# A graph-attention and top-two expert network on one core: one store of routed rows becomes two, and the order of the last work changes

## The chip, the core and the metric

The kernel runs on one core of a Trainium2 chip. The core has five engines that each work through their own list of instructions in order and wait for one another through semaphores: TensorE (PE, with its weight loads shown as PEld), VectorE (DVE), ScalarE (ACT), GpSimd (POOL) and SyncE (SP). SP, ACT and POOL can start DMAs; only POOL starts the indirect ones here, whose rows are addressed by a list of indices. The metric is the device time of one execution in microseconds.

## The reference

The input x has 64 batches of 256 tokens with 256 features, all in f32. Two layers follow each other. Layer 0 is a graph attention with 4 heads over one 256x256 adjacency matrix, and a linear layer. Layer 1 is a graph attention with one head, and a mixture of experts:

```python
x = x + gnn0(layernorm(x), adj)          # 4 heads of 64, leaky relu, masked softmax, elu
x = x + layernorm(x) @ weight.T + bias
x = x + gnn1(layernorm(x), adj)          # one head of 256, relu
t = layernorm(x)                         # tokens of the mixture of experts, 16384 x 256
probs = softmax(t @ router_w.T)          # 8 experts
rw, re = top_k(probs, 2); rw = rw / rw.sum()
x = x + t + sum_e combine[:, e] * (gelu(t @ w1[e] + b1[e]) @ w2[e] + b2[e])
```

Each token needs only the two experts that it chose, so 2 of 8 products have to be computed.

## The kernel before

**Batches.** `batch_layers` handles one batch: both attentions, the linear layer, the norms and the router's logits (the last PE work of a batch, `pl`, L771). A loop at the end of the kernel starts a new batch every three steps and lets all jobs that are alive advance in each step by a rank that they yield. So the order of instructions on each engine is fixed when the program is built. The first instruction of ACT in a batch (L471) and its four matmuls (L463) mark the pace.

**Routing.** The first 61 batches are *routed*, in chunks of 4 batches (eleven times), 2 (seven times) and 1 (three times). For each chunk `route` finds the two best experts of each token (`top_two`), counts by two matmuls (`pp`, L1199 and L1200) how many rows each expert has received so far, and so gives each (token, choice) a row in a store in HBM, `xs`. This store has eight regions, one per expert. `send` (L1155) writes the token's row there with an indirect DMA of POOL, twice per 128 tokens: once for the first choice, once for the second. A row has 260 columns: 256 features, the token's number, the first choice's expert, and the two numbers from which the weight follows.

**Pairs.** A *pair* is two tiles of 128 rows of one region. `allot` decides on DVE which regions have a full pair and writes expert and place of each next pair to a small table; SP, PE and DVE read it into registers. `expert_pair` then runs one pair: SP loads the expert's first weights (`we`, 264 KB, L977), the rows (`xr`, four DMAs, L987) and the last columns (`xt`, L998); DVE turns the rows (L117), PE computes the first product (`ph`, L1050) and ACT the gelu (L1056); DVE picks the weight by comparing the expert's number (L1026, L1030); PE computes the second product (`py`, L1066), DVE adds the bias (L1077) and ACT multiplies by the weight (L1042). The loop starts these jobs from a list, at most about two per batch until late in the kernel.

**Adding.** `scatter` (L1088) adds each of the pair's two tiles to the rows of the output with an indirect, accumulating DMA of POOL. A token's first and second choice may lie in pairs that follow each other, and two accumulating DMAs must not touch one row at the same time. So both scatters of a pair wait for the two of the pair before it (`before = added[-2:] + based`; `based` are the plain stores of the routed batches, which must land first).

**The end.** As a full pair is only certain when a region has 256 rows, E - 1 = 7 pairs are held back. Behind the last chunk `allot_rest` gives out 14 pairs, 10 whole and 4 of one tile; a block of zero rows (`fill`) is written behind each region's last row so that these pairs have defined rows. In all 129 pairs with 254 tiles are computed. The last three batches are not routed but *dense*: `dense_expert` runs all eight experts on a batch, and DVE adds each result by its weight to the batch's sum (L1125), which SP stores (L1136). Their 24 steps are laid between the pairs, in two groups (batch 61, then 62 and 63), and their first weights come from HBM (L1113).

**POOL** also computes the reciprocal roots of the norms (L400, L401, L438, L441), in order with sends and scatters.

**Until batch 18** (`SETTLED`) the layer-0 input is turned by PE and the attention terms of layer 1 by PE too; later DVE and DMAs do this.

## Time and profile before

| | |
|---|---|
| median of 17 runs | 1470.78 us (1466.56 to 1474.3) |
| the profiled execution | 1472.71 us |
| its span, first to last instruction | 1470.6 us |
| mean granted clock of TensorE | 0.985 |
| scatters (L1088) | 254, 407.5 us of POOL |
| sends (L1155) | 244, 256.4 us of POOL |
| product matmuls of experts (L1050, L1066) | 1224 + 1208 records, 280.6 + 282.5 us of PE |
| DMA traffic | 235.14 MB, mean 160 GB/s |

The profile is one execution. Busy time of an engine is the time in which it ran an instruction; register, branch and semaphore instructions are not in it. A PE matmul in f32 shows as two records. "Idle before" in a row is the time that the engine stood still before those instructions, with the work that ended last ahead of them. The clock is the share of full speed that the throttle granted to TensorE.

### The profile page before, as it was taken

The numbers are of one execution on the slowest core, as the hardware profiler recorded it, in microseconds if no ns is written. First come the engines' busy times: TensorE is split into PE (matmuls) and PEld (weight loads), VectorE is DVE, ScalarE is ACT, GpSimd is POOL, SyncE is SP. The second block draws the span as 40 slices with busy tenths as digits, with TensorE's granted clock in tenths as the row PEclk, the third lists the DMA queues.
The fourth block names the chain that finished last, engine by engine and source line by source line (L and its number), as shares of the span: only waits on it lengthen the run. The fifth ranks groups of instructions, "written<-read, shape, count | busy, mean of one in ns | idle before, by whom it ended". The sixth has DMA issues, their size and how long they took to land. (4 is left out here: it accounts for less than half of the span.)

```text
span 1470.6 us, 29780 instructions
## 1 busy us (share of the span) xinstructions
PE 1406.9 (96%) x8030; PEld 1250.9 (85%) x8030; DVE 1235.8 (84%) x4357; ACT 1002.7 (68%) x2385; POOL 856.2 (58%) x849
## 2 busy tenths in 40 slices
PE   6899999999999999999999999999999999889995
PEld 5698888899999999999999999888888888678884
DVE  7789999989998989899999989999888987775443
ACT  1477667677778777777777777766878787653431
POOL 2122446355867676676758585676666677644443
PEclk9899999999999999999999999999999999999998
DMA  4822243567777767787777677668687876799532
GB/s 126 247 81 87 91 131 117 141 163 172 203 182 190 179 165 180 181 196 186 191 170 188 158 196 182 182 166 206 156 197 156 184 158 142 151 224 198 87 44 43
DMA packets 356969, 235.14 MB, mean 160 GB/s; under 512 B 244796, under 2 KB 320068, under 8 KB 356804
## 3 DMA queue, kind: packets, MB, share of 16 engines
q1 hardware_dynamic: 304464, 157.46, 40.6%
q0 software_dynamic: 48288, 65.81, 23.4%
q10 hardware_dynamic: 4052, 9.98, 2.3%
q8 instruction: 66, 1.08, 0.3%
q14 instruction: 99, 0.81, 0.2%
HBM read 145.72 MB, written 87.41 MB: 159 GB/s over the span
## 5 line engine op out<-in xcount | busy, mean ns | idle before, releaser
L1088 POOL DMA_INDIRECT out_dram<-y,xt x254 | 407.5, 1604 | 224.1 <-issue 64.2
L589 PE MATMUL pv<-q,z 128*128 128x65 f32 (+1 forms) x2560 | 363.0, 297 | 0.2
L589 PEld LDWEIGHTS pv<-q,z 128*128 128x128 f32 x2560 | 332.8, 193 | 13.9 <-DVE z L575 0.4
L1155 POOL DMA_INDIRECT xs<-xng,pos x244 | 256.4, 1051 | 65.3 <-issue 58.7
L1066 PE MATMUL py<-w2s,hT 128*128 (+1 forms) x1208 | 282.5, 384 | 5.0 <-ACT hT L1056 5.0
L1066 PEld LDWEIGHTS py<-w2s,hT 128*128 128x128 f32 x1208 | 228.1, 192 | 38.5 <-ACT hT L1056 8.7
L575 DVE SCALAR_TENSOR_TENSOR z<-z,q,mask 128x256 f32<-128x256 f32 x504 | 231.8, 482 | 13.2 <-DMA z<-terms 4.2
L1050 PE MATMUL ph<-sT,we 128*128 128x256 f32 (+1 forms) x1032 | 237.6, 379 | 4.6 <-DVE sT L117 1.7
L1050 PEld LDWEIGHTS ph<-sT,we 128*128 128x128 f32 x1032 | 193.3, 192 | 32.8 <-ACT q L506 2.9
L1042 ACT ACTIVATE y<-y,w 128x256 f32<-128x256 f32 x254 | 111.5, 498 | 114.1 <-DVE y L1077 113.9
L453 ACT COPY xT<-pt 128x512 f32<-128x512 f32 x209 | 121.3, 587 | 84.4 <-PE pt L447 72.5
L400 POOL TENSOR_SCALAR rstd<-mv 128x4 f32<-128x4 f32 (+1 forms) x67 | 15.9, 238 | 212.0 <-DVE mv L378 165.3
L418 ACT ACTIVATE off<-x,sums 128x256 f32<-128x256 f32 x256 | 129.4, 505 | 14.1 <-DVE x L672 8.5
L498 PE MATMUL pq<-wx,xT 128*128 128x259 f32 x512 | 126.1, 389 | 5.4 <-ACT xT L453 5.4
L463 PE MATMUL pq<-wx,xT 128*128 128x268 f32 x512 | 129.3, 396 | 2.1 <-DVE xT L117 0.8
L665 PE MATMUL pf<-wfT,xT 128*128 128x256 f32 x512 | 122.9, 383 | 0.0
L1077 DVE TENSOR_TENSOR y<-py,b2s 128x512 f32<-128x512 f32 (+1 forms) x129 | 84.9, 677 | 44.0 <-PE py L1066 36.2
L1056 ACT ACTIVATE hT<-ph,we 128x256 f32<-128x256 f32 (+1 forms) x258 | 103.3, 469 | 24.4 <-issue 11.2
L463 PEld LDWEIGHTS pq<-wx,xT 128*128 128x128 f32 x512 | 98.7, 193 | 21.8 <-DVE wx L168 1.4
L498 PEld LDWEIGHTS pq<-wx,xT 128*128 128x128 f32 x512 | 96.9, 192 | 22.7 <-ACT xT L453 8.4
L711 ACT ACTIVATE rel<-pv,rinv 128x256 f32<-128x256 f32 x128 | 54.0, 470 | 87.2 <-DVE rinv L596 86.7
L665 PEld LDWEIGHTS pf<-wfT,xT 128*128 128x128 f32 x512 | 93.9, 194 | 10.5 <-ACT xT L453 0.2
(191 smaller groups left out, 2357.2 us busy)
## 6 DMA issues: line engine op xcount, KB each, us to landing
we<-wpack SPq DMA_DIRECT2D x129, 264.0 KB
xr<-xs SPq DMA_DIRECT2D x500, 64.0 KB
z<-terms SPq DMA_DIRECT2D x46, 512.0 KB
xin<-in_x_dram SPq DMA_DIRECT2D x64, 256.0 KB
out_dram<-base SPq DMA_DIRECT2D x61, 256.0 KB
xblk<-in_x_dram SPq DMA_DIRECT2D x188, 64.0 KB
z<-terms ACTq DMA_DIRECT2D x17, 512.0 KB
z<-terms SPq DMA_DIRECT2D x46, 128.0 KB
```

What stands on the lines that cost most here:

```text
L418: nc.scalar.activation(off, src[:, t, :], AF.Square, bias=sums[:, t : t + 1], scale=-float(D), accum_out=sq[:, at + t : at + t + 1],)
L453: nc.scalar.copy(dst, pt)
L463: nc.tensor.matmul(pq.rearrange("p h c -> p (h c)"), xT[:, k, t * P : (t + 1) * P], wx[:, k, :], start=(k == 0), stop=(k == KT - 1),)
L498: nc.tensor.matmul(pq, xT[:, k, t * P : (t + 1) * P], wx1[:, k, :], start=(k == 0), stop=(k == KT - 1),)
L575: nc.vector.scalar_tensor_tensor(z[:, j, :, h, :], terms, q[:, j, h, HD + 2 : HD + 3], masks[0][:, j, :].rearrange("p (t i) -> p t i", t=N ...
L589: nc.tensor.matmul(pv[:, h, :], z(j, h, t), q[:, j, h, : d + 1], start=(j == 0), stop=(j == NT - 1),)
L665: nc.tensor.matmul(pf[:, t, :], xT[:, k, t * P : (t + 1) * P], wfT[:, k, :], start=(k == 0), stop=(k == KT - 1),)
L1042: nc.scalar.activation(y[:, t, :], y[:, t, :], AF.Copy, scale=w[:, t : t + 1])
L1050: nc.tensor.matmul(ph[:, f, :], we[:, k * D + f * P : k * D + (f + 1) * P], xT[:, k, :], start=(k == 0), stop=(k == KT - 1),)
L1066: nc.tensor.matmul(py[:, t, :], hT[:, f, t * P : (t + 1) * P], w2s[:, e, f * D : (f + 1) * D].rearrange("p e c -> p (e c)"), start=(f == 0 ...
L1088: d = nc.gpsimd.indirect_dma_start(out=out_rows, out_offset=bass.IndirectOffsetOnAxis(ap=xt[:, t, 0:1].bitcast(I32), axis=0), in_=y[:, t, ...
L1155: d = nc.gpsimd.indirect_dma_start(out=xs_d[: E * CAP * PAIR, :], out_offset=bass.IndirectOffsetOnAxis(ap=at, axis=0), in_=xe, in_offset=None,
```

## The change

Each choice gets a store of its own, `xs0` and `xs1`, with eight regions each. All tokens' first choices lie in one, all second ones in the other. As each token occurs once in each store, the pairs of one store never share a row: their scatters no longer wait for each other, and only where the choice changes does a scatter wait for those of the other choice. The order in which the two choices are worked through alternates from chunk to chunk, so there is one such change per chunk. A pair's weight lies ready in the row, so the two DVE instructions that picked it are gone; the token's number is written to two columns instead of one.

Each store holds back 7 pairs. There are 62 routed batches and 2 dense ones (one more chunk of 1). Per store 54 pairs are given out as they fill and 15 at the end, 11 whole and 4 of one tile: together 138 pairs with 268 tiles. The filling rows now carry numbers of tokens of the two dense batches, in two columns that alternate between pairs, and are added as zeros; so the scatters of the 30 last pairs wait for both dense stores, and for the last pair but one.

The dense steps begin as soon as a dense batch is routed, two per step of the loop, ahead of the last 30 pairs. The eight experts' first weights are loaded once into the memory that held the attention's z (`bring_home`); dense steps read them there, and each of the last 30 pairs gets its copy by DVE instead of a DMA from HBM. `PAIRED` and `SETTLED` grow by one chunk (to 15 and 22).

```diff
-    CHUNKS = (4,) * 11 + (2,) * 7 + (1,) * 3
+    CHUNKS = (4,) * 11 + (2,) * 7 + (1,) * 4
-    CAP = ROUTED * NT * P // PAIR + 1
+    CAP = ROUTED + 1
+    R = 2 * E
-    PAIRED = CHUNKS[0] + CHUNKS[1] + 3
-    SETTLED = CHUNKS[0] + CHUNKS[1] + CHUNKS[2] + CHUNKS[3] + 2
+    PAIRED = sum(CHUNKS[:3]) + 3
+    SETTLED = sum(CHUNKS[:5]) + 2
...
-    xs_d = tc.dram_tile([(E * CAP + 1) * PAIR, ROW], F32, name="xs")
+    xs_d = [tc.dram_tile([(E * CAP + 1) * PAIR, ROW], F32, name=f"xs{k}") for k in range(2)]
...
-        fill[:, :, D : D + 1].bitcast(I32), pattern=[[1, 2], [1, 1]], base=0,
+        fill[:, :, D : D + 2].bitcast(I32), pattern=[[1, 2], [PAIR, 2]], base=ROUTED * N,
...
-    region = iota([E], [[CAP, E]], 0, 0, "region")
+    region = iota([R], [[0, 2], [CAP, E]], 0, 0, "region")
...
-        z = work.tile([P, NT, NT, H, P], F32, tag="z4", name="z4", bufs=2)
+        z = zbig[:, b % 2]
...
-    def expert_pair(j, n, ids, ef, regs, needs, tiles=2):
+    def expert_pair(k, j, n, ids, regs, needs, tiles=2, at_home=False):
...
-        d = nc.sync.dma_start(
-            out=we, in_=wpack[bass.ds(e_sp, 1), :, :].rearrange("e p c -> (e p) c")
-        )
+        if not at_home:
+            nc.sync.dma_start(
+                out=we, in_=wpack[bass.ds(e_sp, 1), :, :].rearrange("e p c -> (e p) c")
+            )
...
+        if at_home:
...
+            e = bass.ds(regs["copy"][i], 1)
+            nc.vector.tensor_copy(we[:, :C_B1], w1s[:, e, :].rearrange("p e c -> p (e c)"))
+            nc.vector.tensor_copy(
+                we[:, C_B1 : C_B1 + KT], b1s[:, e, :].rearrange("p e c -> p (e c)")
+            )
...
-        nc.vector.scalar_tensor_tensor(
-            w[:, :tiles, None], xt[:, :tiles, 1:2], ef[:, j : j + 1], xt[:, :tiles, 2:3],
-            op0=ALU.is_equal, op1=ALU.mult,
-        )
-        nc.vector.tensor_tensor(
-            w[:, :tiles, None], w[:, :tiles, None], xt[:, :tiles, 3:4], ALU.add
-        )
...
-            nc.scalar.activation(y[:, t, :], y[:, t, :], AF.Copy, scale=w[:, t : t + 1])
-        scatters.append((y, xt))
+            nc.scalar.activation(
+                y[:, t, :], y[:, t, :], AF.Copy, scale=xt[:, t, 2 + k : 3 + k]
+            )
+        scatters.append((k, y, xt, at_home))
...
-        y, xt = scatters.pop(0)
-        before = added[-2:] + based
+        k, y, xt, padded = scatters.pop(0)
+        before = list(based)
+        at = len(rest) % 2
+        if padded:
+            before += [ins for some in rest[-2:-1] for ins in some]
+            rest.append([])
         based.clear()
+        if k != turn[0]:
+            turn[0] = k
+            before += added[1 - k]
+            added[k].clear()
...
-    GROUPS = [range(ROUTED, ROUTED + 1), range(ROUTED + 1, B)]
+    GROUPS = [[b] for b in range(ROUTED, B)]
+    stored = []
+
+    w1s = zbig.rearrange("p a i j h q -> p (a i j h q)").rearrange("p (e c) -> p e c", e=E)
+    b1s = const.tile([P, E, KT], F32, tag="b1s", name="b1s")
+
+    def bring_home():
+
+        for e in range(E):
+            nc.sync.dma_start(
+                out=w1s[:, e, :].rearrange("p (k f) -> p k f", k=KT),
+                in_=w1[e].rearrange("(p k) f -> p k f", p=P),
+            )
+            if e % 2:
+                yield 99
+        nc.sync.dma_start(
+            out=b1s, in_=wpack[:, :, C_B1 : C_B1 + KT].rearrange("e p c -> p e c")
+        )
+        yield 99
...
-            hT = hidden(own["xT"], we)
+            hT = hidden(own["xT"], w1s[:, e, :], b1s[:, e, :])
...
+        stored.append(b)
+        based.append(d.ins)
...
-        m = rt([E, nt], "m")
-        tt(m.rearrange("p e t -> p t e"), ohs[:, 0], ohs[:, 1], ALU.add)
+        m = rt([2, E, nt], "m", 1)
+        vec.tensor_copy(m.rearrange("p k e t -> p k t e"), ohs)
...
+        order_of = (1, 0) if c % 2 else (0, 1)
+        for k in order_of:
             regs = {}
...
+            for j in range(REST if last else n):
+                waiting.append(
+                    lambda k=k, j=j, regs=regs: expert_pair(
+                        k, j, REST if last else n, ids, regs, needs,
+                        1 if last and j >= WHOLE else 2, last,
+                    )
+                )
...
-    FLUSH = 2 * (E - 1)
+    LEFT = ROUTED - max(ROUTED - CHUNKS[-1] - (E - 1), 0)
+    REST = LEFT + E - 1
...
-            done += nt
-            n = max(done - (E - 1) - taken, 0) if b < ROUTED else 0
+            done += nb
+            n = max(done - (E - 1) - taken, 0) if b + nb < ROUTED else 0
...
-                if waiting and len(scatters) < 3:
+                if waiting and len(scatters) < 5:
...
-            if dense_jobs and step >= dense_free:
-                units, job = dense_jobs.pop(0)
-                pairs = waiting or any(a[2].__name__ == "expert_pair" for a in active)
-                dense_free = max(dense_free, step - 0.5) + units * (1.25 if pairs else 0.5)
-                begin(job(), 90)
-            if scatters:
+            for _ in range(2):
+                if dense_jobs:
+                    begin(dense_jobs.pop(0)[1](), 90)
+            if scatters and (len(stored) == DENSE or not scatters[0][3]):
                 def one():
```

`allot` and `allot_rest` become one function that works on both stores at once (arrays of 2 x 8 instead of 8), `top_two` no longer writes the first choice's number to the row, and `route` writes two weights instead of three numbers.

## The prediction

> **What bounds the kernel now.** I read the page first, for the engines and the 40 slices.
>
> ```profile
> span 1470.6 us, 29780 instructions
> PE 1406.9 (96%) x8030; PEld 1250.9 (85%) x8030; DVE 1235.8 (84%) x4357; ACT 1002.7 (68%) x2385; POOL 856.2 (58%) x849
> PE   6899999999999999999999999999999999889995
> PEclk9899999999999999999999999999999999999998
> L1088 POOL DMA_INDIRECT out_dram<-y,xt x254 | 407.5, 1604 | 224.1 <-issue 64.2
> ```
>
> PE is busy 96% of the span, so by the shares everything else is hidden. But shares are means over stages, so I cut the span where the built order of instructions changes character, and asked for each engine's busy time in each stretch.
>
> ```profile
> 73.50:220.60 147.10, 143.75 (x927) 129.59 (x926) 135.06 (x485) 104.69 (x278) 52.25 (x70) 0.99 0.31 97
> 404.40:882.20 477.80, 477.80 (x2824) 433.59 (x2822) 435.16 (x1496) 370.75 (x877) 327.13 (x315) 1.00 0.76 182
> 919.00:1213.10 294.10, 284.49 (x1618) 250.78 (x1616) 262.30 (x959) 224.16 (x501) 200.33 (x188) 1.00 0.76 176
> 1213.10:1312.70 99.60, 87.50 (x418) 73.51 (x417) 74.53 (x358) 67.52 (x159) 65.80 (x58) 0.91 0.78 171
> 1312.70:1455.70 143.00, 139.99 (x658) 121.32 (x658) 71.87 (x178) 49.66 (x118) 62.90 (x40) 1.00 0.59 106
> ```
>
> Columns: stretch, length, then busy time of PE, PEld, DVE, ACT, POOL, granted clock, DMA. In 404-882 PE has no hole. In 919-1213 it lacks 9.6 us, in 1213-1313 12.1 us at a clock of 0.91. From 1312.7 on (the last router matmul of the last batch, L771) nothing is left but expert pairs and dense batches, and PE is full again until 1455.7. Then come 14.9 us without PE. The chain of waits ends there with scatters alone, so I read POOL and PE in order of time in that last stretch.
>
> ```profile
> 1408.33 1.56 POOL L1088 DMA_INDIRECT out_dram<-y,xt  x1 [3.04 <-ACT y L1042]
> 1410.20 1.56 POOL L1088 DMA_INDIRECT out_dram<-y,xt  x1 [0.30 <-issue]
> 1414.72 1.56 POOL L1088 DMA_INDIRECT out_dram<-y,xt  x1 [2.96 <-DMA out_dram<-y,xt]
> 1416.58 1.56 POOL L1088 DMA_INDIRECT out_dram<-y,xt  x1 [0.30 <-issue]
> ...
> 1458.13 1.56 POOL L1088 DMA_INDIRECT out_dram<-y,xt  x1 [2.90 <-issue]
> 1462.66 1.56 POOL L1088 DMA_INDIRECT out_dram<-y,xt  x1 [2.97 <-issue]
> ```
>
> ```profile
> 1422.57 1.99 PE L1066 MATMUL py<-w2s,hT 128*128 128x256 f32 x8 [0.56 <-ACT hT L1056]
> ...
> 1426.92 1.99 PE L1066 MATMUL py<-w2s,hT 128*128 128x256 f32 x8 [0.62 <-ACT hT L1056]
> ```
>
> See three prices. Two scatters that do not wait stand 1.87 us apart (1.56 of POOL, 0.30 to the next). A pair that waits for the pair before it adds 3 us: 6.4 us a pair, 4.5 us for a half pair. And a dense step whose second product follows its own first one costs PE 4.35 us, where a pair or dense step with other work between costs 3.62 (16 matmul records in 3.62 us at 1440.83). The old tail is two balanced lines: PE with 24 dense steps laid between the pairs, and a scatter chain at 6.4 us a pair that POOL crawls along.
>
> **The change, part by part.** The built orders give the counts.
>
> (1) *Two stores, pairs start a chunk later.* Each store holds back E-1 = 7 pairs, so 14 are held instead of 7. In the old order batch 15 carries the first pair and two pairs a batch start at 20; in the new one they start at 19 and 24, and from there to batch 62 batch b+4 carries what batch b did. So four batches with pairs become four without, plus one pair more at the start. The activations that start a batch (L471) give the pace.
>
> ```profile
> 222.70 0.46 ACT L471 ACTIVATE q<-pq,rstd 128x12 f32<-128x12 f32 x2
> 285.76 0.46 ACT L471 ACTIVATE q<-pq,rstd 128x12 f32<-128x12 f32 x2
> 384.49 0.45 ACT L471 ACTIVATE q<-pq,rstd 128x12 f32<-128x12 f32 x2
> 463.55 0.45 ACT L471 ACTIVATE q<-pq,rstd 128x12 f32<-128x12 f32 x2
> ```
>
> These are batches 15, 19, 24 and 28. With pairs four batches take 79.1 us. Without, 4 x 14.45 (batches 5 to 15, 78.2 to 222.7) or 4 x 15.8 (15 to 19, which has sends and a pair in it); I take 15.1, as sends are now there but no pair: 60.4, and 3.7 for the extra pair. Gain 15.0, ends 12.3 and 17.6. The longer use of TensorE transposes (until batch 22) is inside these rows. In the saturated stretch nothing else moves.
>
> (2) *Routing and weights on DVE.* The two instructions per pair that pick the weight go (L1026 and L1030: 0.21 + 0.16 us). Routing gets arrays twice as wide: by the rows 0.03 to 0.1 us more on some ten instructions and three small ones more at 0.17, about 0.6 a chunk. With two pairs a batch that is some 0.4 us less DVE per batch. Under a saturated PE it is worth nothing; in 919-1213, where DVE is busy 89%, 12 batches x 0.4 = 5, of which I take 3. Ends: nothing, and the 9.6 us that PE lacks there. PE's two prefix matmuls double in width (0.05 us a chunk): hidden in rounding.
>
> (3) *Scatters of one choice do not wait for each other.* Where PE is saturated the 3 us were on POOL alone; the norm instructions queued behind them on POOL cost ACT 3.4 us (L471 <- rstd) in the whole span. So nothing until 1313. In 1213-1313 one more batch is routed (four more sends at 1.05, some 25 small DVE instructions): I take 0, ends +4 and -12 (all PE lacks). The last router matmul then comes at 1312.7 - 15 - 3 = 1294.7.
>
> (4) *Dense first.* After that matmul the new PE order is: 5.4 us of old pairs, then eight times two dense steps, each product right behind its own first half, with half of a pair's work from two pairs between groups. 16 x 4.35 + 7 x 3.62 + 5.4 = 100.3, so the last dense product ends at 1395. What is queued behind that: 5 of the 30 remaining pairs have run on PE, and none of their scatters is out, for they are placed behind both dense stores (their filler rows point into those batches). DVE's last accumulations and the store's issue took 2.4 us behind the last product in the old tail (1455.7 to 1458.1); a landing takes about 4 (scatters 3.7 to 4.5). First remaining scatter: 1401.6. POOL has then stood idle for some 60 us.
>
> (5) *The remaining 30 pairs.* They hold 22 whole pairs and 8 halves: 52 scatters. They wait only for the pair before the last. For whole pairs that has landed (4.5 us after issue, and two issues take 3.74), so 44 x 1.87 = 82.3. Halves come in two rows of four; every second one waits 4.5, so 8 x 2.25 = 18. POOL runs until 1501.9. PE needs only 17 x 3.62 + 8 x 2 = 78 us for what is left, and is done by about 1473, so the price of PE does not show.
>
> (6) *Weights copied on chip.* 30 loads of 264 KB leave SP's queue, 30 DVE copies of 128x512 come in. Nearest rows: 0.53 (a one-input instruction on 128x512, L150) and 0.70 (stream transpose). With 0.16 for the bias 0.7 to 0.9 a pair beside 1.4 of other DVE work, under POOL's 3.74: hidden by the scatters; without that cover by PE's 3.62. The eight loads from HBM start while the last batches run; I cost them nothing, as PE works on layers until then, and +5 if D1 waits.
>
> The VectorE copy has a price that only a page states. In before no such copy runs in the tail, and scatters took 1.56 there and 1.60 on average. The Trainium skill, "SBUF — State Buffer", section "Who interferes with whom", says that a plain copy in VectorE's two-port mode locks GpSimd out of SBUF for its whole length, and that GpSimd then cannot write descriptors. By the rows the 30 copies add nothing to POOL; by that rule they could add an estimated 30 x 0.53 = 16 us, and the sum would be 1524. No run here shows it yet.
>
> Sum: 1501.9 is when POOL could issue again, so the last scatter starts near 1500.0; from the start of the last scatter to the end the old tail took 7.96 (1462.66 to 1470.6). Span 1508. The profiled execution took 1472.71, 2.1 more than its span, and lies 1.9 above the median of the runs (1470.78); so the median should read **1508**.
>
> **The rivals.**
> A. *PE sets the end*: scatters keep up, because dense work ends earlier or stores land before the pairs pile up. PE after the last router matmul: 41 x 1.81 + 8 x 1.05 first products, 43 x 1.81 + 8 x 0.95 second ones = 168, plus 16 x 0.72 of dense stalls = 179.5; then 0.42 + 0.51 for the last y and 8.3 to the end. 1294.7 + 189 = 1484. For it: PE bounds nearly all of the span today. Against: 52 x 1.87 cannot start before the stores.
> B. *Faster*: PE's holes of 919-1323 (30 us, counting 17 us at half clock as 8.5) come from POOL's waits and go with them: the tail starts 27 us earlier, 1457 where PE sets the end, and still 1481 where POOL does. It decides if the dense stores land by 1360 instead of 1402. Against: the waits in that stretch name DVE and ACT, and POOL's rstd held ACT 3.4 us.
> C. *The chain stays*: overlapped adding lands so late that each pair still waits about 3 us: 22 x 6.4 + 8 x 4.5 = 177, 77 more: 1585. Landings of up to 7.0 us were seen under load, but at this place the page shows a quiet DMA.
>
> **How the numbers follow.** Forecast 0.71 (with bounds: +16 lock, +5 loads, +4 routing; -12 drain, -6 DVE, -3 early: 1490 to 1530), A 0.14, B 0.07, no measurable change 0.02, C and beyond 0.06. The range reaches from just below A's time to the forecast's upper bound: **1480 to 1530**. The likeliest case's own range is 1490 to 1530. What a measurement here can tell is about 0.2%, 3 us. Faster has only B, 0.07; within 0.2% 0.02; slower all others, 0.91.
>
> **What would show it.** Batch starts four places on should come about 15 us earlier; POOL should have a hole of some 60 us before the first remaining scatter, and then stand 1.87 us apart to the end; the end should lie some 8 us behind the last scatter's start while PE has been idle about 30 us. It is wrong if scatters overlap the dense steps, if spacing is far from 1.87, or if the drain around 1213-1313 changes length.

## The result, and the profile after

The changed kernel takes 1516.46 us (median of 8 runs, 1514.01 to 1519.89), the kernel before on the same chip 1470.23 us (47 runs). The ratio is 1.0315, with a 95% interval of 1.0301 to 1.0329: 46 us slower. The forecast was 1508 us, with a range of 1480 to 1530.

The page of the changed kernel, first the engines and slices, then the scatters' line:

```profile
span 1519.5 us, 30093 instructions
PE 1410.6 (93%) x8058; PEld 1251.7 (82%) x8058; DVE 1208.5 (80%) x4178; ACT 1000.0 (66%) x2397; POOL 886.5 (58%) x871
PE   6899999999999999999999999899999987799990
POOL 2122645455576766667675857746776776420776
L1075 POOL DMA_INDIRECT out_dram<-y,xt x268 | 431.1, 1609 | 202.3 <-ACT y L1017 84.3
```

PE has as much to do as before (1410.6 us against 1406.9), but the span is 49 us longer. The last slices say where: POOL falls to 4, 2 and 0 and rises to 7 again, and PE's last slice is empty.

Cut by stage (stretch, length, busy time of PE, PEld, DVE, ACT, POOL, granted clock, DMA share, GB/s), first the changed kernel, then the drain and the last stage of the kernel before:

```profile
404.81:860.00 455.19, 455.19 (x2691) 413.14 (x2690) 402.98 (x1350) 352.54 (x837) 312.73 (x300) 1.00 0.76 182
1181.80:1302.10 120.30, 98.25 (x484) 82.68 (x483) 81.18 (x378) 73.03 (x172) 86.10 (x76) 0.90 0.86 199
1302.10:1402.50 100.40, 90.77 (x393) 74.28 (x394) 45.33 (x108) 29.11 (x71) 19.86 (x13) 0.98 0.35 56
1402.50:1519.50 117.00, 75.14 (x377) 66.03 (x375) 40.48 (x99) 39.20 (x94) 81.95 (x52) 0.84 0.69 96
```

```profile
1203.60:1312.90 109.30, 97.20 (x480) 82.10 (x479) 83.49 (x395) 74.80 (x176) 73.77 (x66) 0.92 0.78 172
1312.90:1470.60 157.70, 139.80 (x657) 121.12 (x656) 73.72 (x182) 49.46 (x118) 66.02 (x42) 0.97 0.56 99
```

Three differences make up the whole. The last batch starts at 1181.8 instead of 1203.6: 21.8 us gained. The drain from there to the last router matmul takes 120.3 instead of 109.3: 11.0 lost. The last stage takes 217.4 instead of 157.7: 59.7 lost. The sum is 48.9, the difference of the spans.

The gain is seen at the batch starts (ACT's first instruction of batches 15, 19, 24, 28 and 63, which in the kernel before stood at 222.70, 285.76, 384.49, 463.55 and 1203.60):

```profile
219.54 0.46 ACT L477 ACTIVATE q<-pq,rstd 128x12 f32<-128x12 f32 x2
280.94 0.46 ACT L477 ACTIVATE q<-pq,rstd 128x12 f32<-128x12 f32 x2
365.49 0.45 ACT L477 ACTIVATE q<-pq,rstd 128x12 f32<-128x12 f32 x2
444.44 0.45 ACT L477 ACTIVATE q<-pq,rstd 128x12 f32<-128x12 f32 x2
1181.78 0.45 ACT L477 ACTIVATE q<-pq,rstd 128x12 f32<-128x12 f32 x2
```

By batch 28 it is 19.1 us, and 14.2 of it come between batches 19 and 24: in batches 19 to 21 the changed kernel's SP loads no pair, the kernel before's two a batch. From batch 28 to batch 50 nothing changes (it is still 19.2), and 2.6 more come up to batch 63.

The loss in the drain is one hole on PE. PE's and SP's instructions in order of time:

```profile
1282.31 3.42 PE L1044 MATMUL py<-w2s,hT 128*128 x8 [0.45 <-ACT hT L1034]
1296.76 3.78 PE L1028 MATMUL ph<-sT,we 128*128 128x256 f32 x8 [11.04 <-DVE sT L118]
1300.34 1.72 PE L777 MATMUL pl<-rT,xT 128*128 128x8 f32 x8
```

```profile
1272.27 14.19 SPq L1242 DMA_DIRECT2D xs<-fill  x16
1288.69 0.35 SPq L955 DMA_DIRECT2D we<-wpack  x1
1289.46 2.26 SPq L960 DMA_DIRECT2D xr<-xs  x4
```

PE waits 11.04 us for the turned rows of pair 105. Its loads stand in SP's queue behind the 16 fills, which hold that queue for 14.19 us (the kernel before has 8 of them, in two groups of 2 us with a pair's loads in between). The matmuls behind the hole run at half speed (3.78 us for what takes 1.89), with a granted clock of 0.50 from 1296.7 to 1305.6.

The last stage in POOL's order of time, and SP's issue of the second dense store:

```profile
1355.05 1.63 POOL L1075 DMA_INDIRECT out_dram<-y,xt  x1 [0.30 <-issue]
1408.12 1.78 POOL L1075 DMA_INDIRECT out_dram<-y,xt  x1 [51.44 <-ACT y L1017]
1410.20 1.55 POOL L1075 DMA_INDIRECT out_dram<-y,xt  x1 [0.30 <-issue]
...
1457.07 1.56 POOL L1075 DMA_INDIRECT out_dram<-y,xt  x1 [0.69 <-issue]
1462.09 1.78 POOL L1075 DMA_INDIRECT out_dram<-y,xt  x1 [3.46 <-ACT hT L1034]
...
1510.95 1.55 POOL L1075 DMA_INDIRECT out_dram<-y,xt  x1 [1.15 <-issue]
```

```profile
1404.53 0.41 SPq L1134 DMA_DIRECT2D out_dram<-dbase  x1
```

This is the picture that the forecast drew: a hole (51 us, where it said some 60), then scatters 1.86 us apart, with few waits, to the end, the last of them 8.55 us before the end, while PE's last product is over at 1482.1. The page names ACT's `y` as the releaser of the 51 us; that `y` had long been ready. The scatter starts 3.6 us after the second dense store was issued, and e1 below shows that the wait is for the dense stores.

### The profile page after: what moved, and what is told of

The parts are those of the page before. It is cut to its first block, busy times and chain, and to the rows that moved or that the text cites. A ratio compares the mean times of both kernels' runs of the same rounds, so it can differ in the third digit from the quotient of the medians.

```text
span 1519.5 us, 30093 instructions
## 1 busy us (share of the span) xinstructions
PE 1410.6 (93%) x8058; PEld 1251.7 (82%) x8058; DVE 1208.5 (80%) x4178; ACT 1000.0 (66%) x2397; POOL 886.5 (58%) x871
## 4 chain that ended last, share of the span: by engine, by line
PE 63%; DVE 20%; DMA 6%; issue 3%; ACT 3%; SPq 2%; POOL 1%; DVEq 0%; POOLq 0%; ACTq 0%
PE pv L595 14%; PE py L1044 14%; PE ph L1028 14%; DVE z L581 5%; PE pq L469 5%; PE pq L504 5%; PE pf L671 4%; PE pt L453 4%; PE pl L777 2%; DMA out_dram<-y,xt 2%; DMA z<-terms 2%; DVE stats L383 1%; DMA terms<-ut 1%; DVE x L678 1%; ACT hT L1034 1%
## 5 line engine op out<-in xcount | busy, mean ns | idle before, releaser
L1075 POOL DMA_INDIRECT out_dram<-y,xt x268 | 431.1, 1609 | 202.3 <-ACT y L1017 84.3
L595 PEld LDWEIGHTS pv<-q,z 128*128 128x128 f32 x2560 | 331.9, 192 | 14.1 <-DVE z L581 0.4
L1155 POOL DMA_INDIRECT xs<-xng,pos x248 | 263.1, 1061 | 65.8 <-issue 61.2
L1044 PE MATMUL py<-w2s,hT 128*128 (+1 forms) x1200 | 285.9, 386 | 14.3 <-ACT hT L1034 14.3
L1028 PE MATMUL ph<-sT,we 128*128 128x256 f32 (+1 forms) x1104 | 255.2, 380 | 13.6 <-DVE sT L118 11.0
L1028 PEld LDWEIGHTS ph<-sT,we 128*128 128x128 f32 x1104 | 207.2, 194 | 43.7 <-DVE sT L118 11.8
L1017 ACT ACTIVATE y<-y,xt 128x256 f32<-128x256 f32 x268 | 118.3, 499 | 135.0 <-DVE y L1055 135.0
L406 POOL TENSOR_SCALAR rstd<-mv 128x4 f32<-128x4 f32 (+1 forms) x67 | 15.9, 238 | 248.3 <-DVE mv L384 196.8
L1055 DVE TENSOR_TENSOR y<-py,b2s 128x512 f32<-128x512 f32 (+1 forms) x138 | 90.3, 671 | 58.3 <-PE py L1044 30.6
L1034 ACT ACTIVATE hT<-ph,we 128x256 f32<-128x256 f32 (+1 forms) x276 | 110.2, 465 | 27.3 <-PE ph L1028 20.4
L118 DVE STREAM_TRANSPOSE sT<-xr 128x512 f32<-128x512 f32 (+1 forms) x138 | 91.9, 684 | 23.3 <-DMA xr<-xs 23.1
```

Of the source, the lines that this page charges most:

```text
L595: nc.tensor.matmul(pv[:, h, :], z(j, h, t), q[:, j, h, : d + 1], start=(j == 0), stop=(j == NT - 1),)
L1028: nc.tensor.matmul(ph[:, f, :], we[:, k * D + f * P : k * D + (f + 1) * P], xT[:, k, :], start=(k == 0), stop=(k == KT - 1),)
L1034: nc.scalar.activation(hT[:, f, :], ph[:, f, :], AF.Gelu, bias=bias[:, f : f + 1])
L1044: nc.tensor.matmul(py[:, t, :], hT[:, f, t * P : (t + 1) * P], w2s[:, e, f * D : (f + 1) * D].rearrange("p e c -> p (e c)"), start=(f == 0 ...
L1075: d = nc.gpsimd.indirect_dma_start(out=out_rows, out_offset=bass.IndirectOffsetOnAxis(ap=xt[:, t, at : at + 1].bitcast(I32), axis=0), in_= ...
L1155: d = nc.gpsimd.indirect_dma_start(out=xs_d[k][: E * CAP * PAIR, :], out_offset=bass.IndirectOffsetOnAxis(ap=at, axis=0), in_=xe, in_offse ...
```

## The experiments

The chips differ: the kernel before took 1485.8 and 1487.0 us on two others, 1469.5 on a third. So the totals are compared as ratios to the kernel before on the same chip, and the mechanisms by the length of a stage in the trace. This table has the stages of all runs in us, measured in one traced execution each: the drain from the start of the last batch to the end of its router matmul; then, counted from that end, the start of the first of the last 52 scatters (24 with one store, 30 in e9), the time to the start of the last, and the whole last stage.

| kernel | ratio (95%) | drain | first at | first to last | last stage |
|---|---|---|---|---|---|
| before | 1 | 109.3 | 69.5 | 80.3 | 157.7 |
| changed | 1.0315 (1.0301, 1.0329) | 120.3 | 106.1 | 102.8 | 217.4 |
| e1_free | 1.0194 (1.0172, 1.0216) | 122.7 | 61.5 | 130.0 | 200.2 |
| e2_two | 1.0223 (1.0197, 1.0248) | 122.8 | 90.1 | 101.8 | 200.5 |
| e3_fills | 1.0247 (1.0221, 1.0273) | 108.3 | 107.9 | 102.7 | 219.2 |
| e4_hbm | 1.0334 (1.0309, 1.0359) | 122.4 | 104.1 | 104.4 | 217.1 |
| e5_chain | 1.0860 (1.0832, 1.0889) | 124.8 | 103.7 | 175.3 | 287.2 |
| e6_all3 | 1.0040 (1.0025, 1.0056) | 107.6 | 54.1 | 124.9 | 187.6 |
| e7_even | 1.0054 (1.0038, 1.0070) | 105.1 | 51.5 | 130.5 | 190.7 |
| e8_d1 | 0.9970 (0.9952, 0.9989) | 107.5 | 65.5 | 102.7 | 176.8 |
| e9_half | 1.0123 (1.0106, 1.0140) | 121.7 | 105.5 | 75.8 | 188.8 |
| e10_late | 0.9944 (0.9927, 0.9961) | 110.2 | 63.7 | 103.1 | 175.5 |
| e11_d0 | 1.0059 (1.0036, 1.0081) | 107.9 | 78.5 | 104.1 | 191.6 |
| e12_one_d1 | 1.0190 (1.0170, 1.0210) | 108.6 | 98.1 | 79.0 | 185.3 |

The theory was: the last stage is lost because 52 scatters stand in one line behind the dense stores. The first four runs take one suspected loss each. They ran on the same chip, and as e4 turned out to change nothing that can be told, it serves as a control for the other three: against its 122.4 and 217.1, e1's last stage is 16.9 us shorter, e2's 16.6, and e3's drain 14.1.

### e1_free: the remaining scatters do not wait for the dense stores

```diff
-        fill[:, :, D : D + 2].bitcast(I32), pattern=[[1, 2], [PAIR, 2]], base=ROUTED * N,
+        fill[:, :, D : D + 2].bitcast(I32), pattern=[[1, 2], [PAIR, 2]], base=0,
...
         stored.append(b)
-        based.append(d.ins)
...
-            if scatters and (len(stored) == DENSE or not scatters[0][3]):
+            if scatters:
```

That batches 0 and 1 are free for this rests on the data: by then all their rows have been added, as each region has had far more than 256 rows.

> The changed kernel with one thing undone: the filler rows of the last 30 pairs name tokens of batches 0 and 1 instead of the two dense batches, so their scatters need not wait for the dense stores. The filler rows still add zeros, and the output is the same. Theory of the forecast (the 51 us in which POOL stands idle before the first remaining scatter are lost, because 103 us of scatters then follow without a gap): four to five of these pairs have their results by the last dense product at 1402.5 us, so 4 to 5 times 3.74 us and the 6 us until the stores have landed go: 21 to 25 us less, about 1493 us (1488 to 1500), and POOL's hole is gone. Rival (PE would end no earlier anyway, the tail being the dense steps and the pairs on PE): PE's own work after the last dense product is 78 us and 8.5 us follow, so never below 1487; if the place at which POOL starts does not matter, no change, 1513 to 1519.

Measured: ratio 1.0194, that is 18 us less (give or take 4 by the two intervals) than the changed kernel's 1.0315 would be on this chip; the last stage is 17.2 us shorter. The hole of POOL is gone:

```profile
1406.17 1.55 POOL L1075 DMA_INDIRECT out_dram<-y,xt  x1 [8.60 <-ACT y L1017]
1408.03 1.62 POOL L1075 DMA_INDIRECT out_dram<-y,xt  x1 [0.30 <-issue]
1418.26 1.55 POOL L1075 DMA_INDIRECT out_dram<-y,xt  x1 [8.61 <-ACT y L1017]
1420.11 1.62 POOL L1075 DMA_INDIRECT out_dram<-y,xt  x1 [0.30 <-issue]
1424.27 1.55 POOL L1075 DMA_INDIRECT out_dram<-y,xt  x1 [2.53 <-ACT y L1017]
```

One pair per 12.08 us now goes out beside the dense steps, four by their end (1320.5 for the end of the router matmul + 100.4 = 1420.9 us). Four times 3.72 and the 2.2 us by which the fifth comes sooner after the last dense product (3.4 instead of 5.6) are 17.1. So the gate is a real loss, and a smaller one than the 21 to 25 expected: the fifth pair has no result yet when the dense steps end. The larger part of the last stage stays, since the dense steps feed POOL with a pair only every 12 us.

### e2_two: dense steps two by two

```diff
             hT = hidden(own["xT"], w1s[:, e, :], b1s[:, e, :])
-            yield -85
+            yield -91
```

> The changed kernel with the order of two dense steps changed: first product, first product, second product, second product, instead of each second product right behind its own first. Theory: each dense step falls from 4.35 us to 3.62 us of PE, 16 times 0.72 = 11.5 us; the dense stores, and with them the first remaining scatter, come that much earlier and the end too: 1505 us (1502 to 1508). Rival (the dense steps' stalls lie beside something else that is late, such as DVE's accumulation before the store): no change, 1513 to 1519.

Measured: ratio 1.0223, 14 us less; the last stage is 16.9 us shorter. PE's order of time in the dense stretch, first the changed kernel, then this one:

```profile
1396.21 1.99 PE L1044 MATMUL py<-w2s,hT 128*128 128x256 f32 x8 [0.56 <-ACT hT L1034]
1398.04 1.89 PE L1028 MATMUL ph<-xT,z 128*128 128x256 f32 x8
1400.55 1.99 PE L1044 MATMUL py<-w2s,hT 128*128 128x256 f32 x8 [0.62 <-ACT hT L1034]
```

```profile
1371.41 3.62 PE L1028 MATMUL ph<-xT,z 128*128 128x256 f32 x16
1374.86 3.62 PE L1044 MATMUL py<-w2s,hT 128*128 128x256 f32 x16
1378.32 1.89 PE L1028 MATMUL ph<-sT,we 128*128 128x256 f32 x8
```

The 0.6 us waits are gone. Two dense steps and half of a pair's work from two pairs now take 10.36 us (from 1361.05 to 1371.41) instead of 12.08, and eight times 1.72 are 13.8. The expected 11.5 was short because a step without a wait takes 3.45 us from start to start (1371.41 to 1378.32 holds two), and not the 3.62 that a row with its last matmul's end shows. Where the other 3 us of the stage come from was not followed up.

### e3_fills: the fills go behind the loads of the last full pairs

```diff
-        if last:
-            ends_at = rt([R], "ends_at", 1, I32)
...
         yield 95
         for t in range(nt):
             for k in range(2):
                 send(k, xng[t // NT][:, t % NT, :], pos[:, k, t : t + 1])
...
+        if last:
+            ends_at = rt([R], "ends_at", 1, I32)
...
         needs = sent[waited[0] :]
```

> The changed kernel with the 16 filling DMAs (L1242, twice as many as before) issued behind the last routed chunk's sends instead of ahead of them, which puts them behind the loads of pairs 105 to 108 in SP's queue. In the changed kernel they hold that queue for 14.19 us, and PE stands still for 11.04 us before the first product of pair 105. Theory: this stall is the reason why the drain took 11 us longer than before; without it the last router matmul and all behind it come 11 us earlier, with up to 4 us more from the slow clock that follows the hole (a first product of 3.78 us instead of 1.89): 1503 us (1500 to 1507). Rival (POOL's backlog of scatters and sends, solid from 1186 to 1290 us, makes these rows late): the hole stays or moves to the next pair, 1513 to 1519.

Measured: ratio 1.0247, 10 us less; the drain is 108.3 us instead of 120.3. PE's waits from 1170 to 1345 us by group (who waits for what, then us in total, times, longest), the costliest group of the changed kernel and the costliest here:

```profile
PE ph L1028 <- DVE sT L118: 11.0, 1, 11.0
```

```profile
PE py L1044 <- ACT hT L1034: 7.3, 7, 2.9
```

The hole has not moved to another pair, though POOL's line of sends and scatters is as dense as before. So the fills on SP's queue (with the loading of their row numbers, which moved along) were the cause of the longer drain, and POOL's backlog was not. That the fills now end later costs nothing: the first remaining scatter stands at 107.9 instead of 106.1, still set by the dense stores.

### e4_hbm: the last pairs' weights from HBM

```diff
-        if not at_home:
+        if True:
             nc.sync.dma_start(
                 out=we, in_=wpack[bass.ds(e_sp, 1), :, :].rearrange("e p c -> (e p) c")
             )
...
-        if at_home:
...
-            nc.vector.tensor_copy(we[:, :C_B1], w1s[:, e, :].rearrange("p e c -> p (e c)"))
-            nc.vector.tensor_copy(
-                we[:, C_B1 : C_B1 + KT], b1s[:, e, :].rearrange("p e c -> p (e c)")
-            )
```

> The changed kernel with one part undone: each of the last 30 pairs loads its weights from HBM, as the other 108 do, and the 30 pairs of copies by DVE are gone; the dense steps still read the weights in SBUF. Theory of the forecast (the copies lie under POOL's 1.87 us a scatter and cost nothing): no change, 1513 to 1519. Rival one (the copies hold up POOL): faster, by as much as 30 times 0.53 = 16 us, 1500; that is also what the Trainium skill, SBUF — State Buffer, section Who interferes with whom, would make of it. Rival two (30 loads of 264 KB collide with rows and scatters): slower by over 5 us.

Measured: ratio 1.0334 against 1.0315, with intervals that overlap; last stage 217.1 against 217.4. Copy or load makes no difference that these runs can tell, as the forecast had it. The 52 scatters as a group, with the copies (the changed kernel, 1402 to 1519) and without (1420 to 1533; columns: line, engine, operation, names, count, busy us, mean ns, idle before):

```profile
L1075 POOL DMA_INDIRECT out_dram<-y,xt x52 | 82.0, 1576 | 73.9 <-ACT y L1017 54.5 <-issue 10.1 <-ACT hT L1034 6.2
```

```profile
L1064 POOL DMA_INDIRECT out_dram<-y,xt x52 | 80.7, 1552 | 76.1 <-ACT y L1006 53.8 <-issue 12.1 <-DMA out_dram<-y,xt 7.4
```

23 of the 30 copies fall into this stretch; the other seven touch no scatter. The copies cost POOL 1.3 us in all, 24 ns a scatter.

### e5_chain: the wait between pairs put back

```diff
-        before = list(based)
+        before = list(based) + prev[-2:]
...
-            before += [ins for some in rest[-2:-1] for ins in some]
...
             added[k].append(d.ins)
+            prev.append(d.ins)
```

> The changed kernel with its core undone: every pair's two scatters wait for the two of the pair before, as in the kernel before, two stores or not. Theory of the forecast (nothing is gained by dropping the chain while PE is full; in the last stage the chain costs 3 us a pair): the last 52 scatters take 22 times 6.4 and 8 times 4.5 = 177 us instead of 103, so 74 us more in the stage behind the last router matmul (217.8 us in the changed kernel) and 0 to 5 us ahead of it: a ratio to the kernel before of 1.08 (1.075 to 1.09). Rival (scatters of the last stage are bound by their own landings and not by the wait): the ratio stays at 1.03. Rival two (the missing chain also brought the 19 us that the changed kernel gains by batch 28): these 19 us go as well, and the ratio is 1.095 or more.

Measured: ratio 1.0860. The last stage is 287.2 us, 69.8 more, and the 52 scatters take 175.3 us (177 expected). The batch starts are unchanged (444.30 for batch 28, 1181.13 for batch 63), so rival two falls as well: the early gain does not belong to the missing wait. That it belongs to the later start of the pairs fits the place where it arises (batches 19 to 24), but was not tried alone. The wait is seen as before:

```profile
1416.17 1.74 POOL L1074 DMA_INDIRECT out_dram<-y,xt  x1 [3.06 <-ACT y L1017]
...
1422.72 1.55 POOL L1074 DMA_INDIRECT out_dram<-y,xt  x1 [2.95 <-DMA out_dram<-y,xt]
```

So the core of the change does what it says: with 30 pairs left to the end it saves 74 us (span 1593.1 against 1519.5), or 80 by the ratios. But the change also makes 30 of what were 14 remaining pairs.

### e6_all3: the three together

The edits of e1, e2 and e3.

> Three single changes together: filler rows that name batches 0 and 1 (no wait for the dense stores), dense steps two by two, fills behind the last chunk's sends. Alone they took 17.6 us and 17.3 us out of the stage behind the last router matmul and 14 us out of the drain ahead of it. Theory (three separate losses): they add up, 108 us of drain and 183 us of last stage, a span of 1473 where the kernel before has 1470.6, ratio 1.000 (0.996 to 1.006). Rival (the first two shorten the same wait, since both let the remaining scatters start earlier): only one of the two counts, 17 us more, ratio 1.012.

Measured: ratio 1.0040, inside the expected range; drain 107.6 and last stage 187.6. The two savings in the last stage add up to 29.8 of 34.1, so they are two losses and not one. Together they give back all of the change's cost but 6 us.

### e7_even: one dense step, one pair

```diff
-            yield -85
+            yield 60
...
-            for _ in range(2):
+            for _ in range(1):
                 if dense_jobs:
```

with the filler rows of e1 and the fills of e3.

> As the three together, but with one dense step per step of the loop instead of two, so that a dense step and a pair alternate on PE, and each dense second product stands behind the next pair's first product. Theory (in the last stage POOL waits while PE does dense steps, and PE while POOL adds): spread evenly, PE's own 16 dense steps and 30 pairs bound the stage, 175 to 179 us behind the last router matmul instead of 183: ratio 0.996 (0.992 to 1.000). Rival (POOL is the bound wherever the dense steps lie, as 52 scatters and their waits take 103 us in any order): the same as the three together, within 0.002.

Measured: ratio 1.0054, the same as the three together within 0.002: the rival's number, though not its 103 us in any order. The last stage is 190.7 us, PE's last product is over 169 us into it, and the line of scatters lasts 182. Spreading the dense steps starts POOL 2.6 us sooner and feeds it more slowly for longer (130.5 us from first to last).

### e8_d1: one dense batch

```diff
-    CHUNKS = (4,) * 11 + (2,) * 7 + (1,) * 4
+    CHUNKS = (4,) * 11 + (2,) * 7 + (1,) * 5
```

on top of the three.

> As the three together, with 63 routed batches and 1 dense one instead of 62 and 2. Eight dense steps go and two more pairs are given out ahead of the end. Theory (the dense steps are no cover for the remaining pairs, which wait on POOL, but time of PE ahead of them): 8 times 3.45 = 27.6 us less in the last stage, some 7 us more for two pairs, 3 to 7 us more drain: ratio 0.986 (0.982 to 0.992). Rival (with one dense batch too little lies between the last sends and the first remaining pairs, and PE waits for rows): a new hole of 10 us or more ahead of these pairs, ratio 0.994 or more.

Measured: ratio 0.9970, faster than the kernel before by 0.1 to 0.5%. The theory's 0.986 was missed. The ratio lies on the rival's side (0.994 or more), but not for the rival's reason: the hole of 10 us or more is not there, and PE's longest wait in the stage is 2.3 us. Eight dense steps, 27.6 us of PE, went, and the last stage became 10.8 us shorter. The stage cut at the first remaining scatter (columns as above):

```profile
1286.90:1352.30 65.40, 63.06 (x291) 54.86 (x291) 37.84 (x103) 23.05 (x57) 37.33 (x26) 1.00 0.85 178
1352.30:1463.70 111.40, 75.93 (x383) 67.46 (x381) 39.24 (x96) 40.50 (x98) 80.96 (x52) 0.86 0.75 104
```

From the first remaining scatter on there is a fixed 111.4 us: 52 scatters with their few waits (102.7) and 8.7 to the end, while PE is busy for 76 of them. My expectation took the time that leaves PE for the time that leaves the kernel. But the first remaining scatter came at 65.5 instead of 54.1, with PE busy for 63.06 of the 65.40 us ahead of it; 21 tiles of earlier pairs are added in that stretch, where e6 has 18. What makes up the 11.4 us was not followed up.

### e9_half: half of the scatters

```diff
-        for t in range(y.shape[1]):
+        for t in range(1 if padded else y.shape[1]):
```

> The changed kernel, with the second tile of each of the 22 whole remaining pairs not added to the output (those rows keep their base value): 30 scatters instead of 52 behind the dense stores, all else as it was. Theory (POOL's line of scatters sets the last stage): the 102.8 us from the first of these scatters to the start of the last shrink to the wait for the pair before the last one, 2.25 us a scatter, 22 times 2.25 + 18 = 67.5 us, so 35 us less; PE's products of the last pair end at 1482 us in the changed kernel, and 8 to 9 us follow, so not below 1490, 29 us less: ratio 1.010 (1.006 to 1.014). Rival (the loading of the pairs' rows, five DMAs a pair on SP, or landings set this pace): under 10 us less, ratio 1.025 or more.

This kernel leaves out the adding of 22 tiles, so it serves for measuring alone.

Measured: ratio 1.0123, 28 us less, with 30 scatters in 75.8 us instead of 52 in 102.8, and a last stage of 188.8. This is the direct evidence that POOL's line sets the changed kernel's last stage: PE's work and the loading of rows were left as they were. It also shows how near PE is behind: its last product is over at 176.9, 12 us before the end.

### e12_one_d1: the kernel before, with one dense batch

```diff
-    CHUNKS = (4,) * 11 + (2,) * 7 + (1,) * 3
+    CHUNKS = (4,) * 11 + (2,) * 7 + (1,) * 5
...
-    GROUPS = [range(ROUTED, ROUTED + 1), range(ROUTED + 1, B)]
+    GROUPS = [range(ROUTED, B)]
```

> The kernel before, with one store, but with 63 routed batches and one dense one instead of 61 and 3. Theory (with one store the chain of scatters, 6.4 us a pair and 4.5 a half pair, bounds the last stage as soon as dense steps go): 19 whole pairs and 4 halves behind the last router matmul take 140 us and 8 follow, 148 instead of 157.9, with some 6 us more drain for two more routed batches: ratio 0.998 (0.993 to 1.006). Rival (PE bounds it, as its 96% busy say): 16 dense steps of 3.6 us go and 4 pairs come, 44 us less, ratio 0.970 (0.965 to 0.980).

Measured: ratio 1.0190. Slower, which neither number had. The reason is the theory's, at a larger size (stretches of the last stage, columns as above):

```profile
1325.00:1445.00 120.00, 99.98 (x464) 86.67 (x464) 57.23 (x174) 42.47 (x103) 56.66 (x39) 0.93 0.77 158
1445.00:1510.30 65.30, 0.10 (x1) 0.00 (x0) 0.85 (x2) 1.01 (x2) 25.80 (x17) 0.50 0.31 36
```

In the last 65 us PE has nothing left, and POOL works 25.8 of them: the chain alone is left. Behind the last router matmul 50 scatters remained and not the 42 that I took from the kernel before, and many waits were 3.3 to 5.2 us long and not 3. So with one store the dense steps lie beside the chain, and to trade two dense batches for four more pairs in the chain makes it worse; with two stores it is better to have one dense batch than two (e8 against e6).

### e10_late and e11_d0: how far that goes

Both have the edits of e8, and the fills of the first remaining store at once and the others one by one between the loads. e10 lays its last four dense steps among the remaining pairs, by the edit shown; e11 has no dense batch (six chunks of one).

```diff
             for _ in range(2):
-                if dense_jobs:
+                if dense_jobs and (len(dense_jobs) > 4 or step % 6 == 0):
```

> The kernel with one dense batch, and two further changes of order: the fills of the store whose remaining pairs come first are issued at once (8 of 16) and the others one by one between the loads, and the last four dense steps are laid among the remaining pairs instead of ahead of them. Theory (POOL's line of 52 scatters bounds the end, so what counts is when its first one can go): first remaining scatter 6 to 10 us earlier, ratio 0.991 (0.987 to 0.995). Rival (PE, which then has all eight dense steps in the same stretch, falls behind POOL): the same as with one dense batch, 0.997, or slower.

> No dense batch at all: all 64 batches routed, fills divided by store as in the run beside it. Theory (dense steps are only time of PE ahead of the remaining scatters): 28 us of PE go, the last sends come one batch later; the first remaining scatter at some 1337 us, 102.8 us of scatters and 8.7 to the end: 1449 to 1455 us, ratio 0.987 (0.983 to 0.993). Rival (the dense steps cover the way of the last rows through sends, fills and loads): PE stands still for 25 us or more after its last ready pair, ratio 0.997 or more.

Measured for e10: ratio 0.9944, inside the expected range, and the fastest of all. But the last stage is 175.5 against 176.8, and the first remaining scatter came 1.8 us sooner, not 6 to 10. The interval (0.9927 to 0.9961) overlaps that of e8 (0.9952 to 0.9989), which ran on another chip. So that its order gains over e8 is not shown; that it is faster than the kernel before is.

Measured for e11: ratio 1.0059, the rival's side. The first remaining scatter came at 78.5, and PE stood still before it, though for less than the rival's 25 us:

```profile
1336.02 3.62 PE L1043 MATMUL py<-w2s,hT 128*128 x16
1351.38 6.00 PE L1027 MATMUL ph<-sT,we 128*128 128x256 f32 x16 [11.73 <-DVE we L1001]
```

With no dense batch nothing covers the way of the last rows through sends, fills and loads: 11.7 and 4.9 us in two holes, and slow matmuls behind them (16 records in 6.00 us instead of 3.62, at a granted clock of 0.61). One dense batch covers that way (in e8 PE never waits over 2.3 us); the second one only delays POOL.

## Why the prediction was right

It was right in the direction and in the mechanism: the forecast's own case came about, 8.5 us above its number, inside both ranges. Point by point:

- **(1) Two stores, pairs a chunk later: 15.0 us.** 19.1 by batch 28, above the upper end of 17.6. Of this 3.2 are there at batch 15 already, ahead of the stretch that the prediction counted; why stays open. From there to batch 28 it is 15.9.
- **(2) Routing and weights on DVE: 3 us.** 2.6 between batches 50 and 63. That DVE's saving makes them was argued, not tried.
- **(3) Scatters that don't wait: nothing until 1313, and 0 in the drain, with ends of +4 and -12.** Nothing until then is right (e5 leaves the batch starts where they are). The drain is the step that failed: +11.0, outside its bounds, and a drain of another length was one of the prediction's own signs of being wrong. The step counted sends and DVE instructions of one more routed batch and left out the fills, which two stores double from 8 to 16. These stand in one row ahead of a pair's loads on SP's queue. e3 shows that this is the whole of it.
- **(4) Dense first: 100.3 us to the last dense product, first remaining scatter 6.6 later.** 100.4 and 5.6. That the first agrees to 0.1 is luck: the first dense product starts 7.0 us behind the router matmul instead of 5.4, and the dense stretch takes 93.5 us instead of 94.9, mainly since a step without a wait costs 3.45 and not 3.62 (e2).
- **(5) 52 scatters.** From the first to the start of the last 102.8, where 98.4 were forecast. The term that was left out is the change of choice in the middle of the 30 pairs, where one scatter waits for all of the other choice (3.46 us idle at 1462.09); about 1 us more is five scatters of 1.74 to 1.79 instead of 1.55. From the last start to the end 8.55, not 7.96. PE idle for the last 37 us instead of the forecast 30.
- **(6) Weights copied on chip: hidden.** e4 shows it. The copy takes 0.38 alone and 0.41 on average, below the 0.53 that the nearest row gave.

The sum: 7.4 from the start (drain +11.0, earlier gain -3.8, rounding), 0.1, -1.0, 4.4 and 0.6 make 11.5, which is 1519.5 against 1508. The earlier gain hides a third of what the drain lost. The profiled execution itself took 1521.59 us, 5 above the median, so the median is 8.5 above the forecast.

The rule of the Trainium skill that was weighed there ("SBUF — State Buffer", section "Who interferes with whom") would have made an estimated 16 us of the copies. This case has 1.3, and by its rows neither side holds the other for its whole length: copies begun 0.26 and 0.94 us into a scatter took 0.38 us and left it at 1.55. Five scatters that began while a copy was running took some 0.2 us longer each, 1.1 of the 1.3 us. Here the measurement decides.

Of the rivals, *PE sets the end* (1484) was reached by none of the edits e1, e2 and e3 alone; with the three together (e6, 1475.4) POOL's line still ends the kernel, 26 us behind PE's last product. *Faster* named 1360 for the dense stores as the point from which it decides; they landed by 1408. *The chain stays* (1585) is what e5 built, with 1596.

## What to carry to other kernels

When work is rearranged so that an engine no longer waits between its own steps, look at when its first step of the last stage can start and how many steps are then left: 52 steps of 1.87 us behind a gate cost more than 24 in a chain of 3 us waits that ran beside other work. Work of the bounding engine that is "cover" for a slow chain becomes delay once the chain is gone, so its amount has to be chosen again (two dense batches 1.0040, one 0.9970, none 1.0059, the last with the fills divided by store as well). And every queue that a doubled step passes counts, also the one that only issues DMAs.

## What the runs showed of the hardware

- Copies of VectorE and scatters of GpSimd hold each other up, in both directions, at a few moments of a scatter only. In the changed kernel a copy that was running when a scatter started (begun up to 0.2 us ahead) made it 1.74 to 1.79 us long instead of 1.55; a copy that began 0.54 us into a scatter took 0.75 us itself instead of 0.38. Copies at most other moments left both at about their usual length. The other ten runs that keep these copies agree: of 34 copies begun 0.54 to 0.89 us into a scatter 33 ended about 1.28 us after its start, after 0.40 to 0.75 us, while all 48 begun 0.10 to 0.45 us into one took 0.38 to 0.43. VectorE and GpSimd in order of time, in the changed kernel:

```profile
1462.06 0.38 DVE L1001 COPY we<-z 128x512 f32 x1
1464.15 0.38 DVE L1001 COPY we<-z 128x512 f32 x1
```

```profile
1462.09 1.78 POOL L1075 DMA_INDIRECT out_dram<-y,xt  x1 [3.46 <-ACT hT L1034]
1464.17 1.79 POOL L1075 DMA_INDIRECT out_dram<-y,xt  x1 [0.30 <-issue]
1466.27 1.55 POOL L1075 DMA_INDIRECT out_dram<-y,xt  x1 [0.30 <-issue]
```

  Without the copies (e4) no scatter of the last 52 took more than 1.62 us. The kernel before has two of 1.73 and 1.79 in its last stage, beside other instructions of VectorE, so copies are not the only ones that do this.
- Sixteen fills of 260 KB in a row held SP's queue for 14.19 us, 0.89 us each; the kernel before's eight, in two groups of four, took 1.99 and 2.33, some 0.54 each. In e3, where the sixteen come later, they took 14.07. What the length depends on was not tried.
- After a hole of 11 us PE's matmuls took twice their time (3.78 us instead of 1.89 for eight records, then 3.76) until 1305.6, at a granted clock of 0.50; from there on the clock was 0.98 and more. This hole thus cost some 4 us more than its length.
